# Moving one small fetch in a transfer queue: row maxima in front of the next group's loads

## The chip, the cores and the metric

The kernel runs on one core of a Trainium2 chip. The metric is the device time of one execution in microseconds; the program before took 11431.28 us (median of 3 runs, 11428.13 to 11438.58).

## What is computed

A stack of four graph layers over 3327 nodes with 128 features. Layer 0, where the change lies, is attention of an unusual kind: `q`, `k` and `v` are reshaped so that the 128 features act as 128 heads, each with an inner width of 8, and the weighted adjacency matrix is added twice to the scores.

```python
q = (x @ Wq.T).reshape(d, n, h)      # d = 128 heads, n = 3327, h = 8
k = (x @ Wk.T).reshape(d, n, h)
v = (x @ Wv.T).reshape(d, n, h)
a = jnp.einsum('dnh,dmh->dnm', q, k) * scale
a = a + spatial_encoding + edge_encoding     # both are adj
a = jax.nn.softmax(a, axis=2)
out = jnp.einsum('dnm,dmh->dnh', a, v).reshape(n, h * d) @ Wo.T
...
h = jnp.maximum(_layernorm(x, axis=-1), 0.0)
x = x + layer(h, adj)                 # layers 1 to 3: each a product with adj, and pointwise work
```

## The kernel before

**Tiling of the attention.** Queries are cut into 7 column blocks of up to 476 (`NC`, `CW`), heads into 32 groups of 4 (`NG`), keys into 26 tiles of 128, taken in 13 pairs (`NQ`). The main loop (L790) goes through all `pairs`: block by block, in it group by group, in it pair by pair. A *group* in this text is one such group of four heads in one block: 13 pairs, 224 groups in all. For a pair and a head, VectorE writes the adjacency values into PSUM (`seed`, L660), TensorE adds the scores on top (`scores`, L666), ScalarE takes the exponential out of PSUM (`exps`, L678 for two banks at once, L681 for one), and TensorE sums the exponentials times the values into `po` (`values`, L719). In pairs 0, 4 and 8 VectorE makes one of the exponentials itself (L692 to L703). At a group's end VectorE copies `po` out (L727), some way into the next group's pairs since the sums lag behind the scores.

**The order is written out by hand.** The loop runs over slots, four to a pair; what is emitted in a slot goes in that order into each engine's own queue. Between the engines only semaphores order. Transfers to and from memory are nearly all issued by SyncE (SP), one after the other from its queue; a transfer that must wait holds back everything behind it in that queue. By the program's own waits, a transfer of SP also waits for the one eight before it, so no more than eight are under way.

**The next group's loads.** At pair 1 of a group `loads` (L733) puts the next group's 41 transfers into SP's queue: keys `KT` (L564, 16 transfers), queries `QS` (L566 and L568, 24), values `VR` (L581, one). There are two buffers of each of KT, QS and VA. At pair 4 GpSimd negates queries (L576), spreads the values into `VA` (L586), and reads one column of KT (`seen`, L590) as a sign that all is there; the first scores of the next group wait for `seen`.

**The squares.** Softmax needs a bound of each row's scores, and the row maximum of the adjacency is part of it. So, while the attention of block `c` runs, the loop also prepares the squares of 128 adjacency rows that block `c + 1` needs: 22 of them, one every seven groups (`plan_squares`, L761). Four groups in a row load 32 rows each (`rows`), transpose them into `cols` (L293) and take maxima of row pieces into `rm` (L297, the last in the pair before the fifth group). Then in the fifth group, at pairs counted from its start:

- pair 0, `gather` (L310): SP stores `rm` to `rowmax_d` in four transfers (L312)
- pair 3, `back` (L315): SP fetches it as `four`, four pieces of each row side by side (L317)
- pair 7, `finish` (L319): VectorE takes the maximum of the four (L321), adds `bmax` (L322), and SP stores the bounds `b` (L323)
- pair 8, `store`: SP writes the transposed square (L300); pair 10, `spread`: SP fetches the bounds for all partitions (L304)
- in the next group GpSimd subtracts them (`shift`, L307)

What `plan` put down for a pair is emitted in the pair's first slot (L804), ahead of the call of `loads` for that pair (L822):

```python
if at == 0 and i > 0:
    for f, a in behind.pop(i // 4, ()):
        f(*a)
...
if at == 0 and 0 <= i // 4 < n:
    loads(i // 4)
```

The first four squares are made ahead of the loop in another way and are not touched by the change.

Of the kernel before, what the change touches and what calls it, by code (L numbers as in the profile page):

```python
# [85 lines left out]
def squares_of(c):  # L86

    return 0 if c < 0 else -(-min(CW * (c + 1), NP) // P)
# [3 lines left out]
def gnn_kernel(ctx: ExitStack, tc: tile.TileContext, x, adj, Wq, Wk, Wv, Wo, embed, layer,  # L92
# [246 lines left out]
    with tc.tile_pool(name="a1", bufs=1) as a1, tc.tile_pool(name="a2", bufs=2) as a2, \  # L339
# [23 lines left out]
        for t0 in range(0, NT, 2):  # L363
            for s in "kq":
# [3 lines left out]
                for i in range(2):  # L368
                    t = t0 + i
                    sq = a4.tile([P, H, P], F32, name="sq")  # L370
# [167 lines left out]
    with tc.tile_pool(name="e1", bufs=1) as e1, tc.tile_pool(name="e_adj", bufs=30) as e_adj, \  # L538
# [76 lines left out]
        with tc.If(loose < 1), tc.manual_schedule():  # L615
# [117 lines left out]
            def loads(u):  # L733

                c, g, q = pairs[u]
                k = c * NG + g
                if k + 1 < NC * NG:
                    nxt = divmod(k + 1, NG)
                    if q == 1:
                        load_qk(*nxt)  # L740
                        v_of[k + 1] = load_v(*nxt)
                    if q == 4:
                        negate_q(*nxt)
                        spread_v(*nxt, v_of.pop(k + 1))
                        here[k + 1] = all_here(*nxt)
                if c + 1 < NC and (g, q) == (0, 0):
                    plan_squares(c)
                if g == NG - 1 and c + 1 < NC:
                    if q == 0:
                        shift_of[c + 1] = load_shift(c + 1)  # L750
                        adj_of[c + 1] = []
                    while len(adj_of[c + 1]) < min(NT, 2 * q + 6):
                        adj_of[c + 1].append(load_adj(c + 1, len(adj_of[c + 1]), shift_of[c + 1]))
# [4 lines left out]
            def plan(u, f, *a):  # L758
                behind.setdefault(u, []).append((f, a))

            def plan_squares(c):  # L761
                for k, s in enumerate(range(squares_of(c), squares_of(c + 1))):
                    sq, u = Square(e_t, s), (c * NG + 7 * k + 1) * NQ
                    for j in range(4):
                        plan(u, sq.load, j)
                        plan(u + 7, sq.turn, j, 0)
                        plan(u + 11, sq.turn, j, 1)
                        plan(u + 12, sq.largest, j)
                        u += NQ
                    for k, f in ((0, sq.gather), (3, sq.back), (7, sq.finish), (8, sq.store), (10, sq.spread)):  # L770
                        plan(u + k, f)
                    for k in range(NQ):
                        plan(u + NQ + 5 + k, sq.shift, 2 * k, 2 * k + 2)
                    plan(u + 2 * NQ + 6, sq.store, shifted_by_tile)
# [281 lines left out]
    with tc.tile_pool(name="g1", bufs=1) as g1:  # L1056
# [19 lines left out]
        f = sm.div(sm.artanh(yn, L1_MAX_TANH), yn)  # L1076
# [33 lines left out]
    with tc.tile_pool(name="h1", bufs=1) as h1:  # L1110
# [14 lines left out]
        f = sm.mul(sm.div(sm.artanh(pn, L2_MAX_TANH), pn), pf)  # L1125
# [97 lines left out]
```

## Time and profile before

| | |
|---|---|
| median of 3 runs | 11431.28 us (11428.13 to 11438.58) |
| the profiled execution, its own time | 11439.36 us |
| its span, first to last instruction | 11437.2 us |
| ScalarE busy | 10117.7 us, 88% |
| TensorE busy (matmuls) | 10803.1 us, 94% |
| VectorE busy | 8338.7 us, 73% |
| GpSimd busy | 2054.9 us, 18% |
| mean granted TensorE clock | 0.969 |
| attention loop | 515.6 us (first copy of sums) to 10477.9 us (last) |

Shares of the span mix stages with different limits. Ahead of the loop lie projections, behind it the other layers; only inside it do squares and groups run side by side. Matmuls overlap each other and their ends are modelled, so TensorE's 94% doesn't say that it is at its peak.

The profile's chain, followed back from the last instruction, has this on its shares by engine and by line:

```profile
ACT 42%; PE 37%; issue 7%; DMA 5%; DVE 4%; SPq 1%; POOL 0%; DVEq 0%; POOLq 0%; ACTq 0%
ACT e L678 35%; PE po L719 17%; PE S L666 14%; ACT e L681 7%; PE pu L1016 5%; DMA QS<-qS_d 2%; DMA KT<-kS_d 2%; DVE S L660 1%; DVE e L701 1%; DMA four<-rowmax_d 1%; PE pu L968 0%; SPq L564 0%; DVE OS L727 0%; DMA ot<-oT_d 0%; DVE xs L1003 0%
```

SPq is SP's queue, "issue" is time in which an engine waited for nothing that the profile shows. Three kinds of transfers show with 2, 2 and 1% of the span.

### The profile page before, as it was taken

The page shows a single profiled execution, that of the slowest core. Times are in us where ns is not written, and L with a number is a line of the kernel's source. Part 1 is how long each engine was busy: PE and PEld are TensorE (multiplying, and loading weights), DVE is VectorE, ACT ScalarE, POOL GpSimd, SP SyncE. Part 2 cuts the span into 40 slices and gives each one's busy share as a digit, 9 for nine tenths or more (in the row PEclk, how much of TensorE's full clock was granted, in tenths as well). Part 3 has the DMA queues.
Part 4 walks back from the last instruction along what each step waited for, and adds up shares of the span by engine and source line. Part 5 has one row for each costly group of instructions (what it writes and reads, how often), then busy time and mean ns, then how long its engine had stood idle before and what let it go on. Part 6 is the DMA issues. An engine that isn't in the chain of part 4 may idle for free.

```text
span 11437.2 us, 205561 instructions
## 1 busy us (share of the span) xinstructions
PE 10803.1 (94%) x72980; PEld 3659.9 (32%) x72980; DVE 8338.7 (73%) x13563; ACT 10117.7 (88%) x13718; POOL 2054.9 (18%) x3417
## 2 busy tenths in 40 slices
PE   4599999999999999999999999999999999998779
PEld 2133333333333333333333333333333333334444
DVE  5577777777777777777777777777777777777633
ACT  3599999999999999999999999999999999996220
POOL 5211211111112111121111111121111111111000
PEclk7799999999999999999999999999999999999889
DMA  8755555555555555555555555555554544444447
GB/s 244 247 94 98 92 96 113 98 94 91 100 109 100 95 90 92 103 99 95 89 100 110 97 92 97 95 116 94 91 99 85 108 79 84 82 81 126 155 176 272
DMA packets 732443, 1280.87 MB, mean 112 GB/s; under 512 B 190462, under 2 KB 607750, under 8 KB 714908
## 3 DMA queue, kind: packets, MB, share of 16 engines
q1 hardware_dynamic: 689528, 1138.10, 51.2%
q0 software_dynamic: 41888, 129.51, 3.8%
q8 instruction: 591, 9.68, 0.4%
q14 instruction: 436, 3.57, 0.1%
HBM read 1082.90 MB, written 184.09 MB: 111 GB/s over the span
## 4 chain that ended last, share of the span: by engine, by line
ACT 42%; PE 37%; issue 7%; DMA 5%; DVE 4%; SPq 1%; POOL 0%; DVEq 0%; POOLq 0%; ACTq 0%
ACT e L678 35%; PE po L719 17%; PE S L666 14%; ACT e L681 7%; PE pu L1016 5%; DMA QS<-qS_d 2%; DMA KT<-kS_d 2%; DVE S L660 1%; DVE e L701 1%; DMA four<-rowmax_d 1%; PE pu L968 0%; SPq L564 0%; DVE OS L727 0%; DMA ot<-oT_d 0%; DVE xs L1003 0%
## 5 line engine op out<-in xcount | busy, mean ns | idle before, releaser
L678 ACT ACTIVATE e<-S 128x952 f32<-128x952 f32 (+1 forms) x9408 | 8761.8, 1180 | 172.0 <-PE S L666 170.2
L719 PE MATMUL po<-e,VA 128*9 128x476 f32 (+1 forms) x46592 | 5767.2, 567 | 19.4 <-DVE OS L727 1.1
L660 DVE COPY S<-a 128x476 f32<-128x476 f32 (+1 forms) x5824 | 3814.1, 655 | 1994.3 <-ACT e L678 1521.1
L666 PE MATMUL S<-QS,KT 64*128 64x476 f32 (+1 forms) x23296 | 4869.7, 452 | 188.9 <-DVE S L660 178.3
L666 PEld LDWEIGHTS S<-QS,KT 64*128 64x128 f32 x23296 | 2435.1, 184 | 5333.6 <-issue 1642.7
L681 ACT ACTIVATE e<-S 128x476 f32<-128x476 f32 (+1 forms) x3808 | 2432.5, 791 | 36.8 <-PE S L666 36.3
L701 DVE SCALAR_TENSOR_TENSOR e<-e,h 128x476 f32<-128x476 f32 (+1 forms) x2016 | 1395.6, 692 | 46.1
L731 POOL DMA_DIRECT2D oT_d<-OS x896 | 471.7, 532 | 4911.6 <-DVE OS L727 4828.1
L719 PEld LDWEIGHTS po<-e,VA 128*9 128x9 f32 x46592 | 691.2, 88 | 1586.8 <-issue 1495.1
L576 POOL TENSOR_SCALAR QS<-QS 32x476 fp32r<-32x476 f32 (+1 forms) x1344 | 853.4, 635 | 1368.9 <-DMA QS<-qS_d 724.9
L692 DVE TENSOR_SCALAR h<-S 128x476 f32<-128x476 f32 (+1 forms) x672 | 438.5, 653 | 82.0 <-PE S L666 10.9
L701 DVE SCALAR_TENSOR_TENSOR e<-h 128x476 f32<-128x476 f32 (+1 forms) x672 | 451.5, 672 | 0.0
L696 DVE TENSOR_TENSOR h<-h,h 128x476 f32<-128x476 f32 (+1 forms) x672 | 440.4, 655 | 0.0
L703 DVE SCALAR_TENSOR_TENSOR e<-e,h 128x476 f32<-128x476 f32 (+1 forms) x672 | 435.8, 649 | 0.0
L134 ACT COPY uT<-pu 128x494 f32<-128x494 f32 (+1 forms) x12 | 6.6, 546 | 427.3 <-PE pu L1016 427.3
L586 POOL COPY VA<-VR 128x832 f32<-128x832 f32 x224 | 198.8, 888 | 966.7 <-DMA VR<-v_d 687.5
L1016 PE MATMUL pu<-strip,h 128*128 128x494 f32 (+2 forms) x728 | 293.9, 564 | 38.9 <-ACT h L949 38.9
L694 DVE TENSOR_SCALAR h<-h 128x476 f32<-128x476 f32 (+1 forms) x672 | 306.2, 456 | 23.2
L1016 PE MATMUL pu<-strip,y 128*128 128x494 f32 (+2 forms) x728 | 295.5, 568 | 29.0 <-DVE y L1003 18.0
L698 DVE TENSOR_SCALAR h<-h 128x476 int32<-128x476 f32 (+1 forms) x672 | 288.1, 429 | 22.9
L307 POOL TENSOR_TENSOR cols<-cols,on_all 128x256 f32<-128x256 f32 x286 | 249.4, 906 | 0.2
L293 DVE STREAM_TRANSPOSE cols<-rows 128x416 f32<-128x416 f32 x208 | 203.7, 984 | 21.6 <-DMA rows<-in_adj_dram 14.1
(186 smaller groups left out, 2445.8 us busy)
## 6 DMA issues: line engine op xcount, KB each, us to landing
KT<-kS_d SPq DMA_DIRECT2D x1792, 208.0 KB
KT<-kS_d SPq DMA_DIRECT2D x1792, 104.0 KB
VR<-v_d SPq DMA_DIRECT2D x224, 416.0 KB
strip<-adjT POOLq DMA_DIRECT2D x39, 1663.5 KB, 7.3
strip<-adjT SPq DMA_DIRECT2D x36, 1663.5 KB
QS<-qS_d SPq DMA_DIRECT2D x3072, 14.9 KB
QS<-qS_d SPq DMA_DIRECT2D x1536, 29.8 KB
adjT<-cols SPq DMA_DIRECT2D x26, 1664.0 KB
```

Source lines behind the costliest of these rows:

```text
L576: nc.gpsimd.tensor_scalar(QS[b][r0:r0 + 32, j + 1, :w], QS[b][r0:r0 + 32, j, :w].bitcast(F32), -1.0, 0.0, op0=ALU.mult, op1=ALU.add)
L660: touch(u, [r], nc.vector.tensor_copy(bank(u, r), adj_of[c][2 * q + r][:, :w]))
L666: x = nc.tensor.matmul(bank(u, r), KT[b][64 * r:64 * r + 64, max(0, j - 1), q * P:(q + 1) * P], QS[b][64 * r:64 * r + 64, j, :w], start=Fa ...
L678: touch(u, (0, 1), nc.scalar.activation(e[:, :, :w], S[:, odd:even + 1, :w], AF.Exp, scale=2.0))
L681: touch(u, [r], nc.scalar.activation(e[:, 1 - r, :w], bank(u, r), AF.Exp, scale=2.0))
L692: touch(u, [1], nc.vector.tensor_scalar(f, bank(u, 1), LOG2_E2, EXP_LEAST, op0=ALU.mult, op1=ALU.max))
L696: nc.vector.tensor_tensor(f, f, whole, op=ALU.subtract)
L701: nc.vector.scalar_tensor_tensor(e, f if k == 4 else e, EXP_C[k], f, op0=ALU.add, op1=ALU.mult)
L703: nc.vector.scalar_tensor_tensor(e, e, EXP_C[0], power.bitcast(F32), op0=ALU.add, op1=ALU.mult)
L719: nc.tensor.matmul(po[32 * j:32 * j + H + 1, :w], VA[k % 2][:, 2 * pairs[v][2] + of, j, :], e_of[v, j][:, 1 - of, :w], start=(q == 0 and r ...
L731: nc.gpsimd.dma_start(oT_d[:, d * N + c * CW:d * N + c * CW + w], o[32 * j:32 * j + H + 1, :w])
L1016: nc.tensor.matmul(pu[c][:, :w], y[:m, t, :], s[:m, c * AW:c * AW + w], start=(t == 0), stop=(t == NT - 1))
```

## The change

One number in the plan of a square: `back` is emitted at pair 1 in place of pair 3. As `loads` emits the next group's transfers at pair 1, and planned work of a pair comes before it, the fetch now stands in SP's queue directly behind the four stores of `gather` and in front of the 41 loads; before, it stood behind them.

```diff
@@ -767,7 +767,7 @@
                         plan(u + 11, sq.turn, j, 1)
                         plan(u + 12, sq.largest, j)
                         u += NQ
-                    for k, f in ((0, sq.gather), (3, sq.back), (7, sq.finish), (8, sq.store), (10, sq.spread)):
+                    for k, f in ((0, sq.gather), (1, sq.back), (7, sq.finish), (8, sq.store), (10, sq.spread)):
                         plan(u + k, f)
                     for k in range(NQ):
                         plan(u + NQ + 5 + k, sq.shift, 2 * k, 2 * k + 2)
```

The queues of TensorE, VectorE, ScalarE and GpSimd keep their order. In SP's queue 22 transfers (L317) move up by 41 places. `back` reads what `gather` writes, so SP holds it until the four stores are complete, and with it the loads behind it.

## What I expected before the run

> **What bounds the kernel now.** I read the page's busy row, then the waits of each engine, then the timelines of SP's queue, VectorE and ScalarE around one of the waits, and last the busy times by stretch. In the middle of the program (the attention loop, 515 to 10478 us) ScalarE is the engine that never rests, and this table of four stretches shows it. The first is the stall's lead-in; the other three are three head groups in a row, cut at the copy of their sums out of PSUM (L727). Columns: length, then busy time and count of PE, PE's loads, VectorE, ScalarE and GpSimd, granted clock, DMA share, GB/s.
>
> ```profile
> 676.50:690.70 14.20, 14.20 (x106) 4.42 (x98) 11.27 (x18) 14.20 (x20) 0.00 (x0) 1.00 0.58 58
> 690.75:741.30 50.55, 45.52 (x314) 14.30 (x314) 33.53 (x56) 44.12 (x61) 7.05 (x12) 0.93 0.71 119
> 741.30:785.80 44.50, 43.54 (x313) 13.53 (x313) 35.03 (x54) 43.81 (x62) 17.00 (x23) 1.00 0.49 81
> 785.80:829.60 43.80, 43.80 (x315) 14.19 (x312) 32.83 (x55) 43.80 (x61) 8.36 (x15) 1.00 0.64 128
> ```
>
> An undisturbed group is 43.80 us long with ScalarE busy for 43.80 of them: its exponentials are the pace. The group from 690.75 takes 50.55 us for the same work, with ScalarE idle for 6.43. The waits name the cause (us in total, times, longest):
>
> ```profile
> DVE b L321 <- DMA four<-rowmax_d: 154.6, 22, 8.3
> ACT e L678 <- PE S L666: 170.2, 84, 7.9
> ACT e L681 <- PE S L666: 36.3, 11, 6.9
> ```
>
> VectorE stands still 22 times, once for each square of 128 adjacency rows that the loop prepares, until the fetched row maxima `four` land. Behind the standing L321 in its queue are the seeds of PSUM (L660); without them PE has no scores, and ScalarE no exponentials. One such place, SP's queue first, then VectorE, then ScalarE:
>
> ```profile
> 678.87 1.75 SPq L312 DMA_DIRECT2D rowmax_d<-rm  x4
> 680.72 0.82 SPq L564 DMA_DIRECT2D KT<-kS_d  x2
> ...
> 707.71 0.39 SPq L581 DMA_DIRECT2D VR<-v_d  x1
> 708.15 0.51 SPq L317 DMA_DIRECT2D four<-rowmax_d  x1
> ...
> 711.28 0.16 DVE L321 TENSOR_REDUCE b<-four 128x1 f32<-128x4 f32 x1 [5.91 <-DMA four<-rowmax_d]
> ...
> 714.01 0.96 ACT L678 ACTIVATE e<-S 128x952 f32<-128x952 f32 x1 [5.00 <-PE S L666]
> 716.36 8.83 ACT L678 ACTIVATE e<-S 128x952 f32<-128x952 f32 x10 [1.38 <-PE S L666]
> ```
>
> The maxima are stored at 678.87. Their fetch comes after 41 loads of the next group (16 KT, 24 QS, 1 VR), whose issue takes from 680.72 to 708.10, and lands 3.1 us later, at about 711.25. VectorE had reached L321 at 711.28 - 5.91 = 705.37. The loads themselves are early: nobody on the path waits for them here. So the bound is ScalarE, except that 22 times the order of SP's queue is.
>
> **What the Trainium skill says.** "DMA: Bandwidth & Descriptors", section "Two DMAs through the same engine are not ordered", says that a DMA that reads what an earlier DMA wrote needs the issuing engine to wait for the earlier one's completion. So a fetch put right behind the store doesn't ride along with it: SP must stop. Before, the store had landed long since when the fetch came, and SP's own waits show 1.1 us for this in all; how long it must be now I take from below. The same page, "Anatomy of one DMA — SWDGE (gpsimd) path", gives about 2.0 us fixed for a DMA, mostly completion. These DMAs are SP's, and the trace says 3.1 us for `four` and more under load, so I use the trace. "Perfetto Trace Analysis", section "Optimization Strategy", says to look for the gaps of the engine that one optimizes for and what ends them: here 6.43 us of ScalarE's idle time in a group, the currency of all that follows.
>
> **The change part by part.** No instruction is added or removed. On SP's queue the 22 fetches move ahead of 41 transfers each (22 x 41 = 902 places); PE, VectorE and GpSimd keep their order. The four fetches ahead of the loop aren't touched.
>
> *The stall that goes.* I added ScalarE's idle time from one L727 copy to the next for the 22 groups that hold an L321. It is 176.7 us: 0.16 in the last one and 6.4 to 9.8 in the other 21 (mean 8.41). It checks against the waits above: 170.2 + 36.3 = 206.5 us in all, of which some 10 us lie at the loop's start, 8.2 us around 8508 (below), and the rest are gaps below 0.9 us elsewhere. ScalarE loses more than VectorE waits (154.6 us) because PE, too, restarts slowly: the second gap of 1.38 us comes after it, and the granted clock in that stretch is 0.93 against 1.00. Against lengths: the 22 groups sum to 1147.5 us, and 22 x 43.80 = 963.6, so 183.9 us too long; the 7.2 us that ScalarE wasn't idle for are exponentials that ran a little longer, and the last group, with nearly no stall, keeps 0.33 us of excess too. I take 178 us as what comes back.
>
> *When `four` lands now.* By the completions in the trace the four stores landed at 685.9 to 686.7, 6.1 to 7.0 us after issue. Then SP issues the fetch (0.5 us) and it lands about 3.1 us later: 690.3. VectorE asks at 705.4. Cover 15 us; nothing of the wait stays.
>
> *What the loads pay.* They start behind SP's wait: 686.7 + 0.5 = 687.2 instead of 680.72, 6.5 us later. But part of that is already paid. In groups without maxima the run from the first KT to VR takes 24.0 us (median of 201); in the 22 it takes 26.9 to 30.9, median 28.8, since the loads shared the DMA engines and the eight outstanding places with the slow stores. So the last issue moves by about 6.5 + 24.0 - 28.8 = +1.7 us; if nothing of that comes back, by +6.5. They are needed when PE begins the next group's scores, for which it waits on `seen` (L590). That point lies 33.7 us after the L727 copy, seen in the one case where PE did wait:
>
> ```profile
> 8498.95 1.86 SPq L312 DMA_DIRECT2D rowmax_d<-rm  x4
> ...
> 8507.04 1.53 PE L666 MATMUL S<-QS,KT 64*128 64x476 f32 x4 [6.20 <-POOL seen L590]
> ```
>
> PE stopped at 8507.04 - 6.20 = 8500.84, and that group's copy was at 8467.11. Measured so, and with the stall taken out, `seen` is ready 9.3 to 17 us ahead of need in the 22 groups (median 10.5): 690.75 + 33.7 - 712.25 = 12.2 in the one shown. A delay of 1.7 to 6.5 us is hidden in each. Were that cover gone, every us beyond it would cost 22 us.
>
> *What else is queued behind SP's wait.* The negations of QS (L576) and the copy of VA (L586) on GpSimd follow the loads and are in the count above. The store of bounds (L323), the transposed square (L300) and the spread (L304) were issued at 712.16, 712.54 and 719.50; they now come behind a VR that is issued at about 710 to 714, so at most some 2 us later, and the next group's loads, at about 724.5, are ahead of need by 15 us. The shifts that use the spread are in the next group. All nothing. The two small VectorE operations, L321 and L322 (0.16 + 0.66 us), stay; an undisturbed group has VectorE busy for 32.83 of 43.80 us, so they fit beside the exponentials.
>
> *What stays.* The stall at 8508, 8.2 us: its loads took from 8457.61 to 8498.84, 17 us more than others, right behind a load of `rows`, and the fetch of that square comes after them. Also the gaps of about half a us in the groups after, beside GpSimd's shifts.
>
> Sum: -178 + 0. The profiled execution took 11439.4 us (span 11437.2), so 11261; the median of the runs shown, 11431.3, is 8.1 below it, which gives 11253.
>
> **Rivals.**
> *A: the loads come too late.* PE waits on `seen` in place of VectorE on `four`. For it: slack of 9.3 us in the tightest, and 6.5 us is the raw delay; stores of 4-byte pieces were slow (6 to 7 us), and the chain of waits gives QS and KT together 4% of the span. Against: the chain follows what ended last in SP's queue, not lost time, and the loads regain most of the delay. With 2 us lost in each of 21 groups: 11253 + 42 = 11295.
> *B: it loses.* The same mechanism, place and wait: slower needs more than 178 / 22 = 8.1 us of PE waiting per square, that is, loads 8.1 + 10.5 = 18.6 us later than now. This decides only if SP stands about 20 us for stores that landed in 7. It would read 11431 + 22 for each us beyond, say 11475 at 20.6.
> *C: nothing moves.* VectorE finds another late input at the same spot (the squares' columns or rows) or `four` lands late after all. No other wait of VectorE in those groups reaches 1 us, and the fetch has 15 us; 11431.
> *D: only VectorE's own wait returns*, and PE's slow restart stays as a toll: 11431 - 155 = 11276. Against: the slow restart follows the idle time and should go with it.
>
> **How the numbers follow.** Forecast 0.80, D 0.07, A 0.08, C 0.02, B 0.03. About 0.2% is what a measurement of this kernel can tell from no change. Likeliest case: gain between 165 and 186 us (6 us for what the loads may add and for runs that differ by 10 us; upward the full 183.9), so 11245 to 11266. To take in D and most of A the range goes to 11295; below, run-to-run differences of some 5 us: 11240. Faster: forecast, D, A: 0.95. Same: C, 0.02. Slower: B, 0.03.
>
> **What would show it.** The row of waits DVE b L321 on `four` near 0 in place of 154.6; SP's queue with L317 between L312 and the first L564, and a wait of about 6 us ahead of it; ScalarE's waits on PE S from 206.5 to about 30; stall groups of about 44 us. Wrong it would be if PE waited on `seen` more than the one time, or if VR in those groups were issued over 9 us later than now.

## The result, and the profile after

The changed kernel takes 11259.1 us (median of 4 runs, 11258.36 to 11260.43), beside 11434.93 us for the kernel before: a ratio of 0.9847, 95% interval 0.983 to 0.9864. The profiled execution's span went from 11437.2 to 11258.3 us, 178.9 less.

The same head group as before, cut at the copy of its sums (L727), with the one after it. Columns as in the table of stretches above:

```profile
692.03:735.85 43.82, 43.39 (x314) 13.46 (x314) 33.94 (x57) 43.82 (x61) 7.02 (x12) 1.00 0.85 139
735.85:780.30 44.45, 43.46 (x312) 13.47 (x312) 34.85 (x54) 43.76 (x62) 17.23 (x23) 1.00 0.52 88
```

The group is 43.82 us long where it took 50.55, and ScalarE is busy for all of it (44.12 of 50.55 before). The granted clock is 1.00 in place of 0.93. The group after it is what it was.

SP's queue at that place (start, length, line, tiles, count), then VectorE's, then what is left of ScalarE's waits on PE and of PE's on the loads:

```profile
680.16 1.75 SPq L312 DMA_DIRECT2D rowmax_d<-rm  x4
687.87 0.38 SPq L317 DMA_DIRECT2D four<-rowmax_d  x1
688.35 0.90 SPq L564 DMA_DIRECT2D KT<-kS_d  x2
...
713.76 0.39 SPq L581 DMA_DIRECT2D VR<-v_d  x1
714.25 0.45 SPq L323 DMA_DIRECT2D bound_d<-b  x1
714.75 0.59 SPq L300 DMA_DIRECT2D adjT<-cols  x1
```

```profile
706.30 0.65 DVE L703 SCALAR_TENSOR_TENSOR e<-e,h 128x476 f32<-128x476 f32 x1
706.86 0.15 DVE L321 TENSOR_REDUCE b<-four 128x1 f32<-128x4 f32 x1
707.05 0.16 DVE L322 TENSOR_TENSOR b<-b,bmax 128x1 f32<-128x1 f32 x1
708.16 1.42 DVE L660 COPY S<-a 128x476 f32<-128x476 f32 x2 [0.95 <-ACT e L678]
```

```profile
ACT e L678 <- PE S L666: 25.9, 39, 2.8
ACT e L681 <- PE S L666: 7.2, 4, 4.8
...
PE S L666 <- POOL seen L590: 5.1, 1, 5.1
```

SP stands from 681.91 to 687.87 for its own four stores, fetches the maxima, and starts the loads. L321 follows the operation before it without a gap, and the row of its waits on `four` (154.6 us in 22 places before) is gone from the list. ScalarE's waits on scores fell from 206.5 to 33.1 us, that is by 173.4. Its busy time fell by 5.7 (from 10117.7 to 10112.0), since the exponentials had run a little longer in the stall groups; together that is the 178.9 to within 0.2. PE still waits for `seen` in one place only, the one near 8508 before (8327 now).

The chain of what ended last, by line, now reads:

```profile
ACT 71%; issue 11%; PE 9%; DVE 3%; DMA 1%; POOL 0%; SPq 0%; DVEq 0%; POOLq 0%; ACTq 0%
ACT e L678 60%; ACT e L681 12%; PE pu L1016 5%; PE po L719 2%; PE S L666 1%; DVE e L701 1%; DVE S L660 1%; PE pu L968 0%; DMA ot<-oT_d 0%; DVE xs L1003 0%; PE pu L991 0%; DVE h L696 0%; PE pu L979 0%; DMA rows<-in_adj_dram 0%; DVE h L698 0%
```

Before, the chain put QS, KT and `four` together at 5% of the span, some 570 us, though 179 us came back. It had followed SP's queue backwards through 41 loads while ScalarE was working next to them. So the chain's shares were no price here; ScalarE's idle time was.

### The profile page after: what moved, and what is told of

Its sections match the earlier page's. It is cut to its first block, busy times and chain, and to the rows that moved or that the text cites. A ratio compares the mean times of both kernels' runs of the same rounds, so it can differ in the third digit from the quotient of the medians.

```text
span 11258.3 us, 205583 instructions
## 1 busy us (share of the span) xinstructions
PE 10755.5 (96%) x72980; PEld 3651.8 (32%) x72980; DVE 8348.1 (74%) x13563; ACT 10112.0 (90%) x13718; POOL 2069.4 (18%) x3417
## 4 chain that ended last, share of the span: by engine, by line
ACT 71%; issue 11%; PE 9%; DVE 3%; DMA 1%; POOL 0%; SPq 0%; DVEq 0%; POOLq 0%; ACTq 0%
ACT e L678 60%; ACT e L681 12%; PE pu L1016 5%; PE po L719 2%; PE S L666 1%; DVE e L701 1%; DVE S L660 1%; PE pu L968 0%; DMA ot<-oT_d 0%; DVE xs L1003 0%; PE pu L991 0%; DVE h L696 0%; PE pu L979 0%; DMA rows<-in_adj_dram 0%; DVE h L698 0%
```

## Experiments

All edits are to the changed kernel. The runs came in two series, each with runs of the kernel before beside it: 11456.3 us in the first series, 11460.7 in the second, above the 11434.9 that stood beside the result; why it differs is open. So ratios to the kernel before are given, and times are compared within a series.

### The plan's pair, or the place in the queue: `pair2`

```diff
-(1, sq.back)
+(2, sq.back)
```

> The fetch is emitted at pair 2: two of the three pairs' distance to the loads' emission are given up in the plan, but in SP's queue it stands behind the 41 loads, as before the change. Theory (the place in SP's queue decides): as before the change, 11435 us within 10, VectorE waiting about 155 us on four in 21 to 22 places. Rival (what counts is that the fetch is planned earlier): a part of the 176 us comes back, a half or more, 11290 to 11350.

Measured: 11457.0 us (12 runs), ratio 1.000 (0.9992 to 1.0009). The waits of VectorE in its profile, and SP's queue:

```profile
DVE b L321 <- DMA four<-rowmax_d: 170.5, 22, 9.6
```

```profile
682.19 1.75 SPq L312 DMA_DIRECT2D rowmax_d<-rm  x4
684.05 0.82 SPq L564 DMA_DIRECT2D KT<-kS_d  x2
...
712.43 0.39 SPq L581 DMA_DIRECT2D VR<-v_d  x1
712.86 0.51 SPq L317 DMA_DIRECT2D four<-rowmax_d  x1
```

With pair 2 in the plan the fetch is where it was before the change: behind VR. The time and the wait are the old ones. Planning it one pair earlier than before gains nothing; between pair 2 and pair 1 lies the whole effect, since `loads` is emitted at pair 1.

The wait here is 170.5 us where the profile before had 154.6, that is 15.9 more. The run from the first KT to VR took 29.3 us (median of the 22), 28.8 in the profile before; over all 22 it took 14.1 us more. The stall is the difference of when the loads are through and when VectorE asks, so small changes of the loads' time show up in it almost whole. That goes with the slower times of the kernel before in these series, though what made the loads slower was not traced.

### Asking later, with the old order of transfers: `late_finish`

```diff
-(1, sq.back), (7, sq.finish), (8, sq.store), (10, sq.spread)
+(3, sq.back), (8, sq.store), (10, sq.finish), (12, sq.spread)
```

> The fetch stays behind the loads (pair 3, as before the change), but VectorE asks for it at pair 10 and not 7; the bounds' spread goes from pair 10 to 12. Theory (the only loss was VectorE asking at 705 for what landed at 711; three pairs are about 10 us): the wait on four is 0, and the time that of the changed kernel, 11259 us within 6. Rival (putting the fetch in front of the loads is itself what helps, by the order of the transfers): 11400 to 11435. If the loads' delay in the changed kernel costs anything, this one is faster by that, 11240 to 11253.

Measured: 11257.99 us (5 runs, 11254.51 to 11264.97), ratio 0.9828 (0.9815 to 0.9842). The fetch goes out behind VR as before the change, and VectorE takes it without waiting:

```profile
714.86 0.51 SPq L317 DMA_DIRECT2D four<-rowmax_d  x1
715.41 1.53 SPq L300 DMA_DIRECT2D adjT<-cols  x1
721.97 0.35 SPq L323 DMA_DIRECT2D bound_d<-b  x1
```

```profile
719.64 2.04 DVE L701 SCALAR_TENSOR_TENSOR e<-e,h 128x476 f32<-128x476 f32 x3
721.60 0.15 DVE L321 TENSOR_REDUCE b<-four 128x1 f32<-128x4 f32 x1
```

So a gain of the same size comes without touching the order of fetch and loads (the changed kernel was not run in this series; in the other its ratio was 0.983). The loss was a demand some 6 to 8 us ahead of the supply; either end can be moved. The rival that the order of transfers helps by itself falls. The edit also puts the large square store (L300) ahead of the small store of the bounds (L323), which matters further down.

### The loads undelayed: `pool_fetch`

```diff
 def back(self, q=nc.sync):
-    nc.sync.dma_start(self.four, rowmax_d[...])
+    q.dma_start(self.four, rowmax_d[...])
...
-plan(u + k, f)
+plan(u + k, f, *([nc.gpsimd] if f == sq.back else []))
```

> The fetch is emitted at pair 1 as in the changed kernel, but into GpSimd's queue, so SP doesn't stop and the loads start right behind the stores. Theory (the loads' delay of about 5 us is hidden whole): 11259 us within 6, seen is ready some 5 us earlier against need than in the changed kernel. Rival A (late loads cost a little in each group): 11259 less 1 to 2 us for each of 21 groups, 11217 to 11238. If GpSimd's standing costs: slower than 11259 by what its stores of sums or negations come late, up to 11300.

Measured: 11261.74 us (5 runs, 11254.07 to 11268.13), ratio 0.9829 (0.9815 to 0.9842). GpSimd waits for the stores and SP goes straight on to the loads:

```profile
685.33 1.75 SPq L312 DMA_DIRECT2D rowmax_d<-rm  x4
687.19 0.83 SPq L564 DMA_DIRECT2D KT<-kS_d  x2
```

```profile
694.10 0.85 POOL L317 DMA_DIRECT2D four<-rowmax_d  x1 [21.73 <-DMA rowmax_d<-rm]
```

The loads start 0.11 us after the stores' issue, 6.4 us in the changed kernel, and the time is the same. The test is smaller than it looks, and than the expectation had it: beside the slow stores the run from the first KT to VR takes 29.6 us (median) and not 25.2, so `seen` comes only 1.9 us earlier than in the changed kernel, not 5 (in `late_finish` 2.8 us earlier). That much of the loads' delay costs nothing that can be seen. Of 1 to 2 us in each of 21 groups, which rival A asked for, there is no sign, and PE waits for `seen` in no other place than the old one in any of these profiles.

### Where the cover ends: `twice`

```diff
-(1, sq.back), (7
+(1, sq.back), (1, sq.gather), (1, sq.back), (7
```

> The stores and the fetch are made twice in a row ahead of the loads, so SP stands about 11.5 us longer (stores issued 1.8, landed 6, fetch 0.4, landed 3.3 us) in each of 22 groups. In the changed kernel seen is ready 2.0 to 9.0 us ahead of need in 21 of these groups (141 us in all), 16 in one. Theory (a cover that ends): PE waits on seen in about 20 groups for 21 x 11.5 - 141 = about 100 us in all, with the slow restart 100 to 130 us of time: 11360 to 11390. Rival (the loads have far more cover than that, or VectorE's or SP's order gives): 11259 within 10.

Measured: 11374.27 us (4 runs, 11362.08 to 11388.77), ratio 0.9929 (0.9914 to 0.9944), 112 us or more above the two kernels of its series without a stall. Who waited for `seen`, and one such place:

```profile
PEld S L666: 110.0, 22
PE S L666: 90.9, 22
```

```profile
684.84 1.75 SPq L312 DMA_DIRECT2D rowmax_d<-rm  x4
692.91 0.38 SPq L317 DMA_DIRECT2D four<-rowmax_d  x1
695.73 1.73 SPq L312 DMA_DIRECT2D rowmax_d<-rm  x4
704.61 0.38 SPq L317 DMA_DIRECT2D four<-rowmax_d  x1
705.09 0.92 SPq L564 DMA_DIRECT2D KT<-kS_d  x2
```

```profile
733.53 1.44 PE L666 MATMUL S<-QS,KT 64*128 64x476 f32 x4 [3.26 <-POOL seen L590]
```

The first KT goes out 20.3 us after the stores began, not 8.2 us as in the changed kernel, so the loads are 12 us later still. PE's 22 waits sum to 90.9 us (one of them is the old place at the square of 31 rows, 5.7 us), where about 100 was worked out from the remaining lead. PE stops 33.5 to 33.7 us after the L727 copy in all 22, where the prediction took 33.7 from a single case. So the lead is real, it is about 7 us, and the mechanism of rivals A and B exists: it only begins further out than the change goes.

### What is left of the exchange: `after_again` and `no_exchange`

The changed kernel once more, unedited:

> The changed kernel once more, beside the next three on one chip. As before: 0.983 to 0.987 of the kernel before, 11259 us where that takes 11435, and about 11275 where it takes 11456.

Measured: 11263.54 us (5 runs, 11261.59 to 11272.46), ratio 0.983 (0.9817 to 0.9844). The 11275 that was expected beside a kernel before of 11456 did not come: that kernel is some 26 us slower here than beside the result, the changed one only 4. So the change is worth 197 us here and 176 beside the result. It seems that the slower part lies in the stall, which the change takes away: the profile of `pair2` is 24.2 us longer than that of the kernel before, and 17.9 of them are ScalarE's idle time in the 22 groups.

```diff
-((0, sq.gather), (1, sq.back), (7, sq.finish), ...)
+((7, sq.finish), (8, sq.store), (10, sq.spread))
...
-nc.vector.tensor_reduce(b, self.four, axis=AX.X, op=ALU.max)
+nc.vector.tensor_reduce(b, self.four if self.s < squares_of(0) else self.rm, axis=AX.X, op=ALU.max)
```

> For the 22 squares of the loop neither the stores nor the fetch of the maxima are made; VectorE takes its maximum over rm itself. This leaves out the exchange between partitions. Theory (the changed kernel has hidden the exchange whole): the same as the changed kernel beside it within 6 us, ScalarE's idle time in the 22 groups 0 in both. Rival (the change left part of the exchange's cost, by SP's wait or by the loads' delay): faster by 10 us or more.

Measured: 11257.46 us (5 runs, 11253.12 to 11258.03), ratio 0.9822 (0.9808 to 0.9835), 6.1 us below the changed kernel of its series. Between the two profiles the attention loop differs by 7.0 us, and 4.7 of them lie in the one group where PE waits on `seen` at the square of 31 rows: 1.8 us in this profile, 5.4 in that of `after_again`. That this isn't the exchange's cost is likely, not shown: `pool_fetch` has the exchange and waited 1.9 us there. So the exchange of the maxima as the change places it is hidden, to within a few us.

### The one stall that stayed: `split_rows` and `split_late`

SP's queue in the changed kernel at the square with 31 rows:

```profile
8277.96 1.29 SPq L288 DMA_DIRECT2D rows<-in_adj_dram  x4
8279.35 6.33 SPq L564 DMA_DIRECT2D KT<-kS_d  x2
...
8289.53 5.14 SPq L564 DMA_DIRECT2D KT<-kS_d  x2
...
8321.61 0.39 SPq L581 DMA_DIRECT2D VR<-v_d  x1
```

```diff
-nc.sync.dma_start(self.rows[32 * i:32 * i + m, :w], adj[n0:n0 + m, i * KW:i * KW + w])
+for p0, p1 in ((0, m),) if m == 32 else ((0, 16), (16, m)):
+    nc.sync.dma_start(self.rows[32 * i + p0:32 * i + p1, :w], adj[n0 + p0:n0 + p1, i * KW:i * KW + w])
```

> The changed kernel, with the one square that has 31 rows loading them as 16 and 15 rows. In the trace of the changed kernel the four loads of 31 rows land one after the other, at 8287, 8292, 8297 and 8306 us, and the loads of keys behind them wait; PE then waits 5 us on seen, and ScalarE is idle for 7.2. Theory (a load of 31 rows goes through one DMA engine, and holds it): the wait is gone, 7 to 8 us faster than the changed kernel beside it. Rival (31 rows cost nothing, the lateness there is from elsewhere): the same.

The same place with the split:

```profile
8280.60 3.45 SPq L289 DMA_DIRECT2D rows<-in_adj_dram  x8
8284.16 0.78 SPq L566 DMA_DIRECT2D KT<-kS_d  x2
...
8309.28 0.39 SPq L583 DMA_DIRECT2D VR<-v_d  x1
```

Measured: 11256.77 us (5 runs, 11253.51 to 11265.06), ratio 0.9824 (0.981 to 0.9837), 6.8 us below `after_again`. (Two lines are added by the edit, so L564 is L566 here.) By the completions in the trace the four loads of 31 rows had landed at 8284.9, 8289.5, 8294.3 and 8299.0, some 4.7 us apart; the times in the expectation were read off too late, by a later transfer's completions. The eight loads of 16 and 15 rows land about 2 us after their issue each, the last at 8285.6. The loads behind them are through 25.1 us after the first KT and not 42.3, and no wait of PE on `seen` is left in this profile. The ranges of the two kernels overlap a little; that the stall is gone is plain from the profile, its 7 us in the time less so. The Trainium skill's page "DMA: Bandwidth & Descriptors", section "Why a DMA increments its semaphore by 16 and not by 1", says that the number of DMA engines for a transfer is the largest up to 16 that divides the slowest dimension of both its sides: for 31 that is one, for 16 and 15 it is 16 and 15. The trace agrees: the four loads of 31 rows land one behind the other, and the semaphore of each takes a single step when it lands, beside one within 0.5 us of the issue; a load of 15 rows gives 15 steps at the landing, one of 16 or 32 rows gives 16.

`split_late` has the same split, with the order of `late_finish`.

> The same split, with the fetch behind the loads and VectorE asking at pair 10 in place of the changed order. Theory (either place of the fetch is hidden whole): the same as split_rows within 4 us. If the loads' delay costs something, this one is faster by it.

Measured: 11250.13 us (5 runs, 11249.95 to 11251.93), ratio 0.9817 (0.9804 to 0.983): the best of all, 13.4 us below the changed kernel of its series and 6.6 below `split_rows`, more than the 4 that was expected. The two profiles differ by 6.7 us, of which only 2.6 lie in the attention loop; 0.7 lie ahead of it and 3.4 behind it, where the two kernels are the same. So no more than the 2.6 can be put down to the place of the fetch. `late_finish` had no such lead on `pool_fetch` that their ranges would show.

## Why the prediction was right, step by step

- *The bound.* The stall groups were 21 places where SP's order, not an engine, set the pace, and the rest of the loop was ScalarE's. Shown: the stall group is 43.82 us long after, and `late_finish` removes the same stall from the other end.
- *The stall's worth, 178 us.* The profile's span fell by 178.9, the medians by 175.8. ScalarE's idle time, and not VectorE's wait of 154.6, was the right measure: rival D, the restart's toll staying, gave 11276 and falls.
- *The fetch.* Worked out: issued 7.8 us after the first store, and landed 15 us before VectorE asks. Measured: issued 7.2 to 8.6 us after it, median 7.8, and landed 15.8 us (median) before L321; no wait there.
- *The loads' delay, +1.7 to +6.5 us.* The start moved by 6.4 us as worked out; the run to VR took 25.2 us (median) and not 24.0. So VR's issue moved by 2.6 us (33.3 after the first store, 30.7 before, medians).
- *The bound store, square store and spread "all nothing".* Right for the time, but a piece was missed. These stores now follow right behind VR, at 714.25 and 714.75 in the queue shown, where before the fetch and VectorE's wait kept them 4 us away. In 7 of 22 groups VR took 5.2 to 9.4 us to land, against at most 3.6 before. The large square store isn't enough for that: in `late_finish` and `split_late` it is issued 1 to 2 us behind VR, but the small store of the bounds 6 us or more behind it, and VR lands within 4.6 us in all 44 places. What the slow cases have in common is the store of the bounds while VR is under way; whether it does this without the large store beside it was not tested. So `seen` moved by 3.6 us in the median and by more in these, and the smallest lead is 1.7 us (0.7 in the profile of `split_rows`), below the 2.8 that the prediction's own worst case leaves (9.3 - 6.5). That this stayed covered was luck, since the term had been put at nothing; in `twice` such groups are the ones with the longest waits (7.0 to 8.8 us).
- *Rival A and B.* PE waits for `seen` in the one old place only, and `pool_fetch`, with `seen` 1.9 us earlier, is no faster: A cost nothing. `twice` shows that its cost begins when the loads come about 7 us later than in the changed kernel.
- *The median* came 6 us above the forecast of 11253. The kernel before was measured 3.7 us higher beside it, and the gain was 2.2 smaller.

## What to carry to other kernels

A small transfer that stands in a queue behind forty others is late by the forty, however early it is planned; look at its place in the queue, not at the time of the plan, and move either the supply in front of them or the demand behind them. Before moving it in front, add up what then waits behind its own wait, and how much lead those loads have; here 7 us of lead stood over a cliff of some 22 us of time for each us beyond (an estimate, one us in each of 22 groups; in `twice` PE's waits of 90.9 us went with 112 us or more of time). Price a stall by the idle time of the engine that sets the pace, not by the waiting engine and not by the chain's share.

## What was not expected of the hardware

- Four stores of 512 bytes in 4-byte pieces took 7.7 us (median over the 22) from the first issue to the last landing in the changed kernel, with nothing issued behind them; 8.4 us with the loads behind them before.
- A load of 416 KB (VR) lands in 3.4 us (median), but in up to 9.4 us where a store of 512 bytes in 4-byte pieces is issued 0.5 us after it and one of 1664 KB 1 us after it. With the 1664 KB alone so close behind, it lands within 4.6 us in `late_finish` and `split_late`.
- Four loads of 31 rows, 101 KB each, held up everything behind them for some 17 us; as 16 and 15 rows, they did not.
